# PSUM as one ring of eight places, and one drain for each pair of score tiles

## The chip, the cores and the metric

The kernel runs on one core of a Trainium2 chip. The metric is the time of one execution on the device, in microseconds; less is better. The kernel before takes 833.33 us, the median of 3 runs (831.85 to 833.4). Five engines work side by side and wait for one another through semaphores: TensorE (PE; its weight loads are listed as PEld), VectorE (DVE), ScalarE (ACT), GpSimd (POOL) and SyncE (SP), which issues most of the transfers. TensorE writes its products to PSUM, which has eight places (banks) of 512 fp32 numbers in each of 128 partitions; VectorE and ScalarE read them from there.

## The reference

All data are fp32; x is 4 batches of 512 tokens of 256 numbers, and the context has the same shape. Two layers follow each other:

```
x = x + tanh(g_xattn[0]) * attention0(layernorm(x), ctx)
x = x + tanh(g_ffn[0])   * ffn0(layernorm(x))        # weights rounded to -1, 0, 1
x = x + tanh(g_xattn[1]) * attention1(layernorm(x), ctx)
x = x + tanh(g_ffn[1])   * ffn1(layernorm(x))        # one of four experts a token
```

Each attention has 16 heads of 16 numbers: scores are q.k / 4, softmax over the 512 keys, then the weighted sum of the values. Layer 0 adds -0.1 |i - j| to the scores; in layer 1 queries, keys and values go through a relu. The part of interest here is the softmax: its maximum over the keys, and the exponentials.

## The kernel before

The attention of both layers is cut into 32 groups (layer, batch, half of the 256 columns, even or odd heads). A group holds four heads, each in a strip of 32 partitions: 16 for the head and some spare ones. A group has four units, so there are 128 units, and every unit does a quarter of two things:

- `maxima(v, pair)`: for one tile of 128 queries, the scores with queries on the partitions and the 512 keys along the row. Its two products, one for each head of the pair, go to two places of PSUM, and VectorE's `tensor_reduce` takes each one's maximum over the keys into a column of `m` (L517).
- `weights(u, pair)`: for one tile of 128 keys, the scores again with keys on the partitions and the 512 queries along the row. The queries carry their negative maximum in a spare row (`shifted` writes it there, from `m` turned by TensorE), so that the products are already shifted. ScalarE's `Exp` takes each of the two places to `p` (L532). In layer 0 GpSimd then multiplies one block by a decay (L535).

`scores(u, vs)` puts these together. A unit's four pairs form two quads: [maxima pair 0, weights pair 1], then [maxima pair 1, weights pair 0]. All four products of a quad are issued to TensorE, then its two drains to VectorE and ScalarE. The four use different strips of TensorE's rows, so they run side by side. The maxima run `LEAD` = 6 units ahead of the weights. A few quads hold two pairs of the same kind.

After each unit's scores `slot(u)` issues other work: every fourth unit `weighted` (the product of the exponentials with the values, L560) and `shifted`; between them jobs from `chains`, lists of steps with due times (projections, layer norms, the hidden layers of the first feed-forward, routing), up to a cost of `SLOT`. The order on TensorE, VectorE, ScalarE and GpSimd is the order in which the code issues the instructions. After the last unit comes the tail with the experts' tiles.

All products, of scores and of everything else, get their place of PSUM from `bank_psum` (L64). It takes a tile of one place from a pool with eight buffers, in turn. The framework that builds the program adds the waits: a product waits until the place's last readers are done, a reader waits for the place's writers, and two engines that read the same place are put in order.

Of the kernel before, what the change touches and what calls it, by code (L numbers as in the profile page):

```python
# [11 lines left out]
F32 = mybir.dt.float32  # L12
U32 = mybir.dt.uint32
AF = mybir.ActivationFunctionType
ALU = mybir.AluOpType
AX = mybir.AxisListType
PSUM = bass.MemoryType.PSUM
ET = mybir.EngineType

P = 128  # L20
# [9 lines left out]
SCALE = 1.0 / np.sqrt(DK)  # L30
# [21 lines left out]
def flamingo_kernel(ctx: ExitStack, tc: tile.TileContext, t: dict, out: bass.AP):  # L52
    nc = tc.nc
# [5 lines left out]
    wts = ctx.enter_context(tc.tile_pool(name="wts", bufs=2))  # L59
    dram = ctx.enter_context(tc.tile_pool(name="dram", bufs=1, space=bass.MemoryType.DRAM))  # L60
    sml = ctx.enter_context(tc.tile_pool(name="sml", bufs=4))
    ps = ctx.enter_context(tc.tile_pool(name="ps", bufs=8, space=PSUM))

    def bank_psum(name):  # L64
        return ps.tile([P, 512], F32, tag="bank", name=name)


    x = [const.tile([P, NT, D], F32, tag=f"x{b}", name=f"x{b}") for b in range(B)]
# [190 lines left out]
    def output_bias():  # L259


        bvm = made["bvm"]
        pb = bank_psum("pbv")[:, 0:D]
        for c in range(NC):
            nc.tensor.matmul(
                pb, lhsT=bvm[:, c, :], rhs=wo0[:, c, :], start=(c == 0), stop=(c == NC - 1)
            )
        nc.vector.tensor_tensor(bo0, bo0, pb, ALU.add)
        nc.gpsimd.tensor_scalar(bo0, bo0, gx0, None, ALU.mult)


    def quantize(flat, name, by_two):
# [12 lines left out]
        def limits():  # L285
            tot = bank_psum(f"qtot_{name}")
            nc.tensor.matmul(tot[:, 0:1], lhsT=ones, rhs=part[:, 0:1], start=True, stop=True)

            mean = sml.tile([P, 1], F32, tag="qmean", name=f"qmean_{name}")
            nc.vector.tensor_scalar(mean, tot[:, 0:1], 1.0 / (D * FF), 1e-5, ALU.mult, ALU.add)  # L290
            nc.vector.tensor_scalar(thr[:, 0:1], mean, 0.5, None, ALU.mult)
            nc.vector.tensor_scalar(thr[:, 1:2], mean, -0.5, None, ALU.mult)
# [82 lines left out]
    def transposed(src, dst, name, alone=False):  # L375

        for c in range(NC):
            pt = bank_psum(f"pt_{name}{c}")
            for n in range(NT):
                nc.tensor.transpose(pt[:, ts(n, P)], src[:, n, ts(c, P)], ident)  # L380
            (nc.scalar.copy if alone or c == 0 else nc.vector.tensor_copy)(dst[:, c, :], pt)
# [119 lines left out]
    def score(out_, lhs, rhs, i, n):  # L501
        r = slice(i * HP, (i + 1) * HP)
        nc.tensor.matmul(out_, lhsT=lhs[r, ts(n, P)], rhs=rhs[r, :], start=True, stop=True)  # L503

    def maxima(v, pair):

        g = groups[v // NT]
        n = v % NT
        pm = [bank_psum(f"pm{v}{pair}{i}") for i in range(2)]
        for i in range(2):  # L510
            score(pm[i], qs[g], ks[g], 2 * pair + i, n)
        m = m_sb[g[0]][g[3]]
        r = SPARE[g[3]]

        def drain():
            for i in range(2):
                nc.vector.tensor_reduce(m[:, n, 2 * pair + i, r : r + 1], pm[i], AX.X, ALU.max)  # L517

        return drain

    def weights(u, pair):

        g = groups[u // NT]
        kt = u % NT
        psc = [bank_psum(f"psc{u}{pair}{i}") for i in range(2)]
        for i in range(2):
            score(psc[i], ks[g], q2s[g], 2 * pair + i, kt)

        def drain():
            p = act.tile([P, 2, S], F32, tag="p", name=f"p{u}{pair}", bufs=10)  # L530
            for i in range(2):
                nc.scalar.activation(p[:, i, :], psc[i], AF.Exp, scale=SCALE)  # L532
            if g[0] == 0:
                d = p[:, :, ts(kt, P)]
                nc.gpsimd.tensor_tensor(d, d, dec.unsqueeze(1).to_broadcast([P, 2, P]), ALU.mult)  # L535
            ps_exp[u, pair] = p

        return drain

    def scores(u, vs):  # L540

        ms = [(maxima, v, pair) for v in vs for pair in range(2)]
        ws = [(weights, u, 1 - pair) for pair in range(2)] if 0 <= u < n_units else []
        while ms or ws:
            if ms and ws:
                quad = [ms.pop(0), ws.pop(0)]
            else:
                left = ms or ws
                quad = [left.pop(0), left.pop(0)]
            for drain in [f(w, pair) for f, w, pair in quad]:  # L550
                drain()
# [712 lines left out]
    for u in range(-NT, n_units):  # L1264
# [22 lines left out]
        if u in totals:  # L1287
            job, i = totals[u]
# [215 lines left out]
```

## Time and profile before

| | |
|---|---|
| median of the runs | 833.33 us |
| profiled execution | 831.85 us, of which the span from first to last instruction is 830.1 |
| mean granted TensorE clock | 0.994 |
| VectorE: maxima, L517 | 512 of 683 ns, 317.0 us |
| ScalarE: exponentials, L532 | 512 of 601 ns, 267.1 us |
| TensorE: score products, L503 | 2048 passes, 263.1 us (maxima) and 275.5 us (weights) |
| TensorE: exponentials with values, L560 | 1024 passes of 595 ns, 116.5 us |
| GpSimd: decay, L535 | 128 of 746 ns, 94.9 us |

The page lists for each group of instructions its line, engine, operation, what it writes and reads, how many there are, then its busy time and the mean time of one, and last the time for which the engine was idle just before, with what ended it. An fp32 product appears as two passes. TensorE's passes overlap, and their ends are modelled, so its busy time may hold short waits; the starts show them.

### The profile page before, as it was taken

The page shows a single profiled execution, that of the slowest core. Times are in us where ns is not written, and L with a number is a line of the kernel's source. Part 1 is how long each engine was busy: PE and PEld are TensorE (multiplying, and loading weights), DVE is VectorE, ACT ScalarE, POOL GpSimd, SP SyncE. Part 2 cuts the span into 40 slices and gives each one's busy share as a digit, 9 for nine tenths or more (in the row PEclk, how much of TensorE's full clock was granted, in tenths as well). Part 3 has the DMA queues.
Part 4 walks back from the last instruction along what each step waited for, and adds up shares of the span by engine and source line. Part 5 has one row for each costly group of instructions (what it writes and reads, how often), then busy time and mean ns, then how long its engine had stood idle before and what let it go on. Part 6 is the DMA issues. An engine that isn't in the chain of part 4 may idle for free. (4 is left out here: it accounts for less than half of the span.)

```text
span 830.1 us, 13595 instructions
## 1 busy us (share of the span) xinstructions
PE 805.9 (97%) x5220; PEld 450.6 (54%) x5220; DVE 565.7 (68%) x1258; ACT 430.2 (52%) x900; POOL 290.5 (35%) x453
## 2 busy tenths in 40 slices
PE   5999999999999999999999999999999999999995
PEld 3444444545454345644565444564444555899994
DVE  6768868765857686577854676557687764689443
ACT  2476655653546454455635566346756666533341
POOL 5548455624233253231011132002313431735722
PEclk9999999999999999999999999999999999999998
DMA  8200000000001000000000001000104222726820
GB/s 313 77 1 1 1 1 1 1 1 1 1 1 39 1 1 1 1 27 1 1 1 1 26 1 52 1 1 1 52 1 148 91 94 77 273 80 240 303 94 32
DMA packets 17712, 42.28 MB, mean 51 GB/s; under 512 B 2032, under 2 KB 12016, under 8 KB 15216
## 3 DMA queue, kind: packets, MB, share of 16 engines
q0 software_dynamic: 5104, 27.34, 9.4%
q1 hardware_dynamic: 12128, 13.54, 4.8%
q8 instruction: 41, 0.67, 0.3%
q10 hardware_dynamic: 416, 0.54, 0.2%
q14 instruction: 23, 0.19, 0.1%
HBM read 35.13 MB, written 6.29 MB: 50 GB/s over the span
## 5 line engine op out<-in xcount | busy, mean ns | idle before, releaser
L517 DVE TENSOR_REDUCE m<-pm 128x1 f32<-128x512 f32 x512 | 317.0, 683 | 109.1 <-PE psc L503 105.6
L532 ACT ACTIVATE p<-psc 128x512 f32<-128x512 f32 x512 | 267.1, 601 | 145.7 <-PE psc L503 143.5
L503 PE MATMUL psc<-q,k 32*128 32x512 f32 x1024 | 275.5, 624 | 0.0
L503 PE MATMUL pm<-k,q 32*128 32x512 f32 x1024 | 263.1, 617 | 1.5 <-ACT q L490 0.9
L535 POOL TENSOR_TENSOR p<-p,dec 128x256 f32<-128x256 f32 x128 | 94.9, 746 | 170.9 <-ACT p L532 170.9
L503 PEld LDWEIGHTS pm<-k,q 32*128 32x128 f32 x1024 | 92.8, 184 | 83.4 <-issue 48.1
L503 PEld LDWEIGHTS psc<-q,k 32*128 32x128 f32 x1024 | 105.7, 184 | 51.4 <-issue 27.7
L560 PE MATMUL po<-p,v 128*32 128x512 f32 x1024 | 116.5, 595 | 0.8 <-DVE m L517 0.8
L560 PEld LDWEIGHTS po<-p,v 128*32 128x32 f32 x1024 | 31.3, 109 | 80.9 <-issue 58.6
L1104 PE MATMUL pg<-xs,wg 128*128 128x128 f32 x608 | 71.6, 276 | 0.7 <-DVE m L517 0.7
L1104 PEld LDWEIGHTS pg<-xs,wg 128*128 128x128 f32 x608 | 69.8, 192 | 4.1 <-DVE m L517 1.7
L583 POOL TENSOR_TENSOR q<-q,mT 128x512 f32<-128x512 f32 x16 | 20.3, 1269 | 132.3 <-ACT mT L582 132.3
L1130 ACT ACTIVATE ha<-pg,wg 128x128 f32<-128x128 f32 x120 | 34.3, 368 | 52.5 <-PE pg L1104 52.5
L682 PE MATMUL ph<-xTf,w1q 128*128 128x512 f32 x128 | 60.0, 605 | 0.0
L566 ACT COPY oT<-po 128x512 f32<-128x512 f32 x32 | 18.7, 586 | 75.6 <-PE po L560 75.6
L1299 PE MATMUL pyf<-wo,ha 128*128 128x256 f32 x256 | 57.6, 379 | 0.0
L388 PE MATMUL py_f<-w2q,h 128*128 128x256 f32 x256 | 57.2, 381 | 0.0
L388 PEld LDWEIGHTS py_f<-w2q,h 128*128 128x128 f32 x256 | 48.0, 190 | 9.4 <-DVE m L517 3.0
L1299 PEld LDWEIGHTS pyf<-wo,ha 128*128 128x128 f32 x256 | 47.6, 190 | 5.9
L460 PE MATMUL pk<-cT,wk 128*128 128x512 f32 x68 | 35.3, 644 | 7.3 <-DMA cT<-in_ctxT_dram 7.3
L682 PEld LDWEIGHTS ph<-xTf,w1q 128*128 128x128 f32 x128 | 22.6, 189 | 30.3 <-issue 18.2
L393 DVE SCALAR_TENSOR_TENSOR x<-py_f,tg,x 128x512 f32<-128x512 f32 x8 | 6.0, 751 | 42.4 <-PE py_f L388 42.4
(259 smaller groups left out, 828.6 us busy)
## 6 DMA issues: line engine op xcount, KB each, us to landing
x<-in_x_dram SPq DMA_DIRECT2D x4, 512.0 KB, 8.5
rows_d<-xn_f SPq DMA_DIRECT2D x4, 512.0 KB, 3.0
rows_d<-x SPq DMA_DIRECT2D x4, 512.0 KB, 3.7
cT<-in_ctxT_dram SPq DMA_DIRECT2D x3, 512.0 KB, 9.6
w1q<-in_w_dram SPq DMA_DIRECT2D x1, 1024.0 KB, 8.8
w2q<-in_w_dram SPq DMA_DIRECT2D x1, 1024.0 KB, 11.2
wo<-in_wo_dram SPq DMA_DIRECT2D x2, 512.0 KB, 3.8
rows<-in_rows_dram SPq DMA_DIRECT2D x1, 640.0 KB, 9.2
```

Of the source, the lines that this page charges most:

```text
L388: nc.tensor.matmul(py[:, n, :], lhsT=operand(c, n0 + n), rhs=w[:, c, :], start=(c == 0), stop=(c == chunks - 1),)
L460: nc.tensor.matmul(pp, lhsT=attn_w[layer][w][:, c, ts(tt, P)], rhs=src[:, c, :], start=(c == 0), stop=(c == NC - 1),)
L503: nc.tensor.matmul(out_, lhsT=lhs[r, ts(n, P)], rhs=rhs[r, :], start=True, stop=True)
L517: nc.vector.tensor_reduce(m[:, n, 2 * pair + i, r : r + 1], pm[i], AX.X, ALU.max)
L532: nc.scalar.activation(p[:, i, :], psc[i], AF.Exp, scale=SCALE)
L535: nc.gpsimd.tensor_tensor(d, d, dec.unsqueeze(1).to_broadcast([P, 2, P]), ALU.mult)
L560: nc.tensor.matmul(po[i * HP : (i + 1) * HP, :], lhsT=v_sb[b % 2][0][:, kt, c0 : c0 + HP], rhs=ps_exp[NT * s + kt, i // 2][:, i % 2, :], s ...
L583: nc.gpsimd.tensor_tensor(q2s[g], qs[g], turned, ALU.subtract)
L682: nc.tensor.matmul(ph, lhsT=w1q[:, c, ts(f, P)], rhs=st["xT"][:, c, :], start=(c == 0), stop=(c == NC - 1),)
L1104: nc.tensor.matmul(ph[:, f, :], lhsT=w[:, c, ts(f2 * NF // 2 + f, P)], rhs=xs[j][:, c, :], start=(c == 0), stop=(c == NC - 1),)
L1130: nc.scalar.activation(ha[:, f, :], (ha if src is None else src)[:, f, :], AF.Gelu, bias=biases[j][:, fa : fa + 1],)
L1299: nc.tensor.matmul(py, lhsT=hs[j, f // 4][:, f % 4, :], rhs=wo1[f // 4][:, f % 4, :], start=(f == 0), stop=(f == NF - 1),)
```

## The change

PSUM becomes one tile, `ring`, of eight places. `bank_psum` hands out the places in turn, as before. `two_banks` takes two in turn and also returns one access pattern over both: two neighbours, or, where the first is place 7 and the second place 0, a pattern over place 0 and place 7 with a step of seven places (the pair is handed out in that order then, so that head and column still match). Each drain is one instruction over the two places: `tensor_reduce` writes two columns of `m`, and `Exp` writes all of `p`.

```diff
-    ps = ctx.enter_context(tc.tile_pool(name="ps", bufs=8, space=PSUM))
+    ps = ctx.enter_context(tc.tile_pool(name="ps", bufs=1, space=PSUM))
+
+    ring = ps.tile([P, 8, 512], F32, name="ring")
+    turn_of = [0]
 
     def bank_psum(name):
-        return ps.tile([P, 512], F32, tag="bank", name=name)
+        i = turn_of[0]
+        turn_of[0] = (i + 1) % 8
+        return ring[:, i, :]
+
+    def two_banks(name):
+
+        i = turn_of[0]
+        both = [bank_psum(name) for _ in range(2)]
+        if i == 7:
+            return both[::-1], ring[:, 0:8:7, :]
+        return both, ring[:, i : i + 2, :]
...
-        pm = [bank_psum(f"pm{v}{pair}{i}") for i in range(2)]
+        pm, both = two_banks(f"pm{v}{pair}")
         for i in range(2):
             score(pm[i], qs[g], ks[g], 2 * pair + i, n)
...
         def drain():
-            for i in range(2):
-                nc.vector.tensor_reduce(m[:, n, 2 * pair + i, r : r + 1], pm[i], AX.X, ALU.max)
+            nc.vector.tensor_reduce(m[:, n, 2 * pair : 2 * pair + 2, r], both, AX.X, ALU.max)
...
-        psc = [bank_psum(f"psc{u}{pair}{i}") for i in range(2)]
+        psc, both = two_banks(f"psc{u}{pair}")
         for i in range(2):
             score(psc[i], ks[g], q2s[g], 2 * pair + i, kt)
...
             p = act.tile([P, 2, S], F32, tag="p", name=f"p{u}{pair}", bufs=10)
-            for i in range(2):
-                nc.scalar.activation(p[:, i, :], psc[i], AF.Exp, scale=SCALE)
+            nc.scalar.activation(p, both, AF.Exp, scale=SCALE)
```

## The prediction

> **What bounds the kernel now.** I read the page's busy shares first, then its clock row and costliest groups.
>
> ```profile
> PE 805.9 (97%) x5220; PEld 450.6 (54%) x5220; DVE 565.7 (68%) x1258; ACT 430.2 (52%) x900; POOL 290.5 (35%) x453
> ...
> PEclk9999999999999999999999999999999999999998
> ...
> L517 DVE TENSOR_REDUCE m<-pm 128x1 f32<-128x512 f32 x512 | 317.0, 683 | 109.1 <-PE psc L503 105.6
> L532 ACT ACTIVATE p<-psc 128x512 f32<-128x512 f32 x512 | 267.1, 601 | 145.7 <-PE psc L503 143.5
> L503 PE MATMUL psc<-q,k 32*128 32x512 f32 x1024 | 275.5, 624 | 0.0
> L503 PE MATMUL pm<-k,q 32*128 32x512 f32 x1024 | 263.1, 617 | 1.5 <-ACT q L490 0.9
> ```
>
> TensorE is busy 97% of the span with almost no idle before its groups; VectorE and ScalarE idle, and what they idle for is the score products (105.6 and 143.5 us). So TensorE sets the time. Its busy time has modelled ends, though, and can hide short waits, so I turned to starts. The timeline of one unit, engine by engine (start, length, group):
>
> ```profile
> 404.26 0.70 PE L503 MATMUL pm<-k,q 32*128 32x512 f32 x2
> 404.28 0.70 PE L503 MATMUL psc<-q,k 32*128 32x512 f32 x2
> ...
> 405.24 0.59 PE L503 MATMUL pm<-k,q 32*128 32x512 f32 x2
> ...
> 406.35 0.70 PE L460 MATMUL pk<-cT,wk 128*128 128x512 f32 x1
> ...
> 405.42 2.48 DVE L517 TENSOR_REDUCE m<-pm 128x1 f32<-128x512 f32 x4 [0.18 <-PE psc L503]
> ...
> 405.56 2.07 ACT L532 ACTIVATE p<-psc 128x512 f32<-128x512 f32 x4 [2.75 <-PE psc L503]
> ```
>
> The first quad of four products starts at 404.26, the second 0.98 later at 405.24, without waiting for the drains of the first, which begin at 405.42 and 405.56 only. The job behind starts at 406.35, 1.11 after the second quad, while both drain engines are still at it. The eight places are what allows that: TensorE runs one unit ahead of its drains. Over all 256 quads the next work starts 0.97 after the quad's start at best; what lies above that sums to 39.5 us. That is all that better drains could give back.
>
> **Part 1: one instruction for two.** 256 reductions and 256 exponentials go (as built, 555 reductions become 299, 784 activations 528). In a row, reductions start every 0.598 us, so a pair took 0.598 + 0.683 = 1.28; the row of 128x512 against the 128x256 rows of VectorE (L1311 421 ns, L585 679 ns) gives about 1.04 ns an element, so one of 1024 elements takes 0.683 + 512 x 1.04 = 1.22. ScalarE: starts every 0.478, a pair 1.08; copies of 256 and 512 elements (389, 586 ns) and of 128 (281) give about 0.8 ns an element, so 0.601 + 0.41 = 1.01. Saved: some 0.06 a pair on each engine, 15 us of busy time each, on engines that are 68% and 52% busy: alone worth nothing on the path but a part of the 39.5 us. Against it the pair's first place comes free with its second, 0.55 later than now. The quad that reuses them mostly needs both; I cost this at nothing, between -10 and +10.
>
> **Part 2: the ring, where the pair is places 7 and 0.** Single places are still taken in turn, so a pair starts at any place. Where it starts at 7, the read is `ring[:, 0:8:7, :]`, whose first and last address enclose the whole ring. I looked up in the built program what each instruction waits for. A read of two neighbours waits for those two places' writers. A read of 7 and 0 is taken to touch all eight: it waits for the last read by the other drain engine, of whatever place, and for the quad's other products; the other drain engine's next read waits for it; and **the next TensorE instruction waits for it, whatever place that one writes**. I counted 65 such pairs, 36 reductions and 29 exponentials, spread over the attention (quads at 32 to 690 us of the span). At each, the unit's overlap above is gone, and TensorE stands until the drain is over. Behind the waiting product stands all of TensorE's queue, the bound of the kernel.
>
> A rule of the Trainium skill bears on this: "PSUM — Partial Sum Buffer", section "PSUM bank collisions raise a hardware error", asks that any two engines' accesses to one bank and quadrant be serialised, ScalarE's against VectorE's reads too. By that rule a wrapped pair would need to be ordered against places 7 and 0 alone, both old by then, and would cost nothing; the built program orders it against all eight. The row in before that shows an order of two readers of one place is `k` L474 waiting for `k` L472: 10.0 us in 8 times. The sum below goes by the program's waits; by the rule alone it would be 0.
>
> The price at the unit shown, with 0.05 us from a drain's end to what it releases (q of L496 ended at 411.71, the product that waited for its place started at 411.76):
> - Reduction of the first quad: 405.42 + 1.22 + 0.05 = 406.69 for the second quad, which started at 405.24: **1.45**.
> - Exponential of the first quad: it waits for that quad's reduction first: 406.69 + 1.01 + 0.05 = 407.75: **2.5**.
> - Reduction of the second quad: after the first (406.64) + 1.22 + 0.05 = 407.91 for the job, which started at 406.35: **1.55**.
> - Exponential of the second quad: 407.91 + 1.01 + 0.05 = 408.97: **2.6**.
>
> I made this sum at all 65 places, each with its own starts in the trace of before: 24 reductions ahead of a quad 36.6 us, 12 ahead of a job 18.4, 15 exponentials ahead of a quad 41.4 (one of 4.6 where VectorE is busy with the routing), 14 ahead of a job 36.3: **+133 us**. Of it comes back: after such a stand all places are free, so the small waits of the quads behind shrink; 29.3 of the 39.5 us lie at quads without a wrapped pair, and I take half, **-15** (between 0 and -29). If a drain of two took as long as two apart, 65 reductions (29 of them ahead of an exponential) and 29 exponentials cost 0.06 more each, +6.
>
> **Part 3: the clock.** Before never stands for long, except at the head, where the windows view shows (stretch, PE, PEld, DVE, ACT, POOL, then the granted clock):
>
> ```profile
> 21.86:25.28 3.42, 3.42 (x22) 1.58 (x15) 2.91 (x6) 2.16 (x5) 3.16 (x13) 1.00 0.99 333
> 25.28:28.69 3.41, 1.47 (x9) 1.16 (x8) 3.37 (x6) 0.00 (x0) 3.19 (x24) 1.00 0.03 6
> 28.69:32.10 3.41, 3.41 (x14) 1.59 (x15) 0.00 (x0) 0.59 (x1) 2.54 (x3) 0.50 0.03 7
> 32.10:35.51 3.41, 3.41 (x22) 1.29 (x15) 3.21 (x6) 3.12 (x8) 1.45 (x2) 1.00 0.00 0
> ```
>
> The reader is to see that TensorE stood 1.94 us of one stretch of 3.41 and ran the next one at half clock: about 1.7 us of work lost. The Trainium skill, "TensorE: Matmul & The Clock Gate", Part 1, lets the clock fall only after an idle window of some 3.4 us; by it no stand here (2.9 at most but for one) costs clock, and the change ends 28 us lower. By the row, a stand of about 2 us inside one stretch suffices. I take the row. A stand of 2.6 is cut by a stretch's boundary into two parts under 1.8 for 1.0 of 3.41 positions, so some 0.7 of them have 1.8 or more in one stretch; one of 1.5 never has. I take 0.65, and 1.5 us lost for each: 29 x 0.65 x 1.5 = **+28**. Ends: 0 by the rule; if stands of 1.5 trip it half the time too, 36 x 0.5 x 1.5 = 27 more.
>
> **What stays.** Order and amount of TensorE's work are the same; no DMA moves; the experts' tail after 690 us takes single places only and costs nothing more. GpSimd's decay (L535, 746 ns) starts after a pair as before.
>
> **Sum.** The profiled execution took 831.85 (span 830.1, so 1.75 around it), the fastest of the three, whose median is 833.33. 831.85 + 133 - 15 + 28 = 978; I say **977**.
>
> **Rivals.**
> - *Same waits, no clock loss.* For it: the skill's rule, and that score products and weight loads around a stand may count as activity. Against: the row above. 831.85 + 133 - 15 = 950.
> - *The stands are largely absorbed.* If most of the 65 waits are satisfied sooner, say because drains start with the quad's first product, half the sum: 831.85 + 66 - 15 = 883. For it: VectorE and ScalarE idle a third and a half. Against: those idle times are waits for the very products; nothing runs ahead of a TensorE that stands.
> - *Not slower.* The mechanism: the drains' saved 0.06 a pair and fewer instructions end the hidden waits at the places' release, 39.5 us at most: 831.85 - 39.5 = 792 if the wrapped reads cost nothing. It decides once a wrapped pair costs under 0.6 us (39.5 / 65). Against: one reduction alone is 1.22, and the instruction behind it on TensorE names it.
> - *The change doesn't do what it says*: the built program has 256 fewer instructions on each engine, so it does.
>
> **Numbers.** Stands with clock loss 0.62 (977, own range 960 to 1010), stands without 0.26 (950, from 935), absorbed 0.08 (883), not slower 0.04. The range 930 to 1020 takes in the first two: its low end is no clock loss with all 29 us back (831.85 + 133 - 29 = 936) and drains a little shorter, its high end nothing back and the clock lost at the short stands too (831.85 + 133 + 28 + 27 = 1020). What a measurement can tell from no change is about 0.2%, 1.7 us; slower than that 0.96, faster 0.03, within 0.01.
>
> **What would show it.** PE's share falls from 97% to some 85%, with idle before its groups, released by `m` and `p`, of 100 us and more; the group of reductions has 256 of about 1220 ns and that of exponentials 256 of about 1010; ScalarE gains a wait of `p` for `m` and VectorE one of `m` for `p`, which the waits view of before does not have; a stretch at half clock after many of ScalarE's wrapped pairs. I am wrong if TensorE's idle stays under 40 us, if the pairs' durations are far from these, or if the mean clock stays at 0.99 (then 950). A time under 834 would refute the stands.

## The result, and the profile after

The changed kernel takes 1022.61 us (median of 5 runs, 1020.23 to 1027.79), the kernel before 832.34 in the same five rounds: a ratio of 1.2289, with a 95% interval of 1.2269 to 1.2308. The forecast was 977 with a range of 930 to 1020: the sign and the place were right, but the time lies just above the range. The profiled execution was the slowest of the five, 1027.79 us with a span of 1026.1; the parts below are of that execution, against the 831.85 of before.

The page of the kernel after, busy shares, clock row (the granted clock in tenths, over 40 equal slices of the span) and the groups that answer to those shown of before:

```profile
PE 848.2 (83%) x5220; PEld 452.4 (44%) x5220; DVE 558.7 (54%) x1002; ACT 421.8 (41%) x644; POOL 289.3 (28%) x453
...
PEclk9999999989899899989999999999999899999998
...
L530 DVE TENSOR_REDUCE m<-ring 128x2 f32<-128x1024 f32 x256 | 305.6, 1222 | 248.6 <-PE ring L517 235.1
L544 ACT ACTIVATE p<-ring 128x1024 f32<-128x1024 f32 x256 | 256.5, 1022 | 272.5 <-PE ring L517 170.6
L517 PE MATMUL ring<-k,q 32*128 32x512 f32 x1024 | 270.5, 639 | 78.5 <-ACT p L544 40.3
L517 PE MATMUL ring<-q,k 32*128 32x512 f32 x1024 | 281.5, 649 | 0.3 <-DVE h L702 0.3
```

The drains of two have the durations of the sum (1222 ns for 1220, 1022 for 1010), and both drain engines are less busy than before. TensorE's busy share has fallen from 97% to 83%, and the products of the maxima now have 78.5 us of idle time in front of them where there were 1.5. The waits view names what ends it (engine and line, what it waited for, total, times, longest):

```profile
ACT p L544 <- DVE m L530: 97.8, 56, 4.2
...
PEld ring L517 <- ACT p L544: 54.1, 20, 5.3
PEld ring L517 <- DVE m L530: 53.8, 27, 2.9
...
PE ring L517 <- ACT p L544: 40.3, 15, 4.5
PE ring L517 <- DVE m L530: 37.3, 26, 2.0
```

The first row, exponentials that wait for maxima, did not exist before: two engines that read different heads' scores now take turns. The others are the score products and their weight loads, which wait for the drains' ends. The timeline of one unit shows the whole chain; its first quad's pair of exponentials lies in places 7 and 0. First the starts of its two quads in the kernel before:

```profile
144.94 0.70 PE L503 MATMUL pm<-k,q 32*128 32x512 f32 x2
...
145.92 0.59 PE L503 MATMUL pm<-k,q 32*128 32x512 f32 x2
```

Then the same unit in the changed kernel:

```profile
173.94 0.70 PE L517 MATMUL ring<-k,q 32*128 32x512 f32 x2
...
174.47 0.59 PE L517 MATMUL ring<-k,q 32*128 32x512 f32 x2
174.49 0.59 PE L517 MATMUL ring<-q,k 32*128 32x512 f32 x2
177.56 0.70 PE L517 MATMUL ring<-k,q 32*128 32x512 f32 x2 [2.48 <-ACT p L544]
...
175.14 1.23 DVE L530 TENSOR_REDUCE m<-ring 128x2 f32<-128x1024 f32 x1 [1.34 <-PE ring L517]
...
176.48 1.02 ACT L544 ACTIVATE p<-ring 128x1024 f32<-128x1024 f32 x1 [1.83 <-DVE m L530]
```

Before, the second quad starts 0.98 us behind the first. Now the first quad's last passes start at 174.47; the reduction runs to 176.37, only then the exponential starts, to 177.50, and the second quad, which writes neither of the two places, starts at 177.56, 3.62 behind the first. The wrapped exponential itself takes 1.02 us, like the others: what costs is the waiting, not the read.

**Where the 196 us went.** I compared, quad by quad, the time from a quad's first start to the start of TensorE's next work in both traces, then the time of the jobs between units. The clock loss is an estimate: time at half clock (a granted clock of 0.5, in stretches of 3.41 us) is priced at 0.42 us per us, which is what the jobs, the same work in both, give: they take 32.3 us more and have 77 us more of half clock in them.

| part | us more than before | of it clock |
|---|---|---|
| 65 quads with a wrapped pair | 137.8 | 2 |
| other second quads and the work behind them (97) | 26.3 | 5 |
| other first quads and the quad behind them (94) | -0.6 | 2 |
| jobs between the units | 32.3 | 32 |
| head and tail | 0.2 | 0 |

So some 136 us are stands (times in which TensorE waits), 19 a loss at quads without a wrapped pair, and 41 the clock.

### The profile page after: what moved, and what is told of

Read it like the earlier page. It is cut to its first block, busy times and chain, and to the rows that moved or that the text cites. A ratio compares the mean times of both kernels' runs of the same rounds, so it can differ in the third digit from the quotient of the medians.

```text
span 1026.1 us, 13209 instructions
## 1 busy us (share of the span) xinstructions
PE 848.2 (83%) x5220; PEld 452.4 (44%) x5220; DVE 558.7 (54%) x1002; ACT 421.8 (41%) x644; POOL 289.3 (28%) x453
## 5 line engine op out<-in xcount | busy, mean ns | idle before, releaser
L530 DVE TENSOR_REDUCE m<-ring 128x2 f32<-128x1024 f32 x256 | 305.6, 1222 | 248.6 <-PE ring L517 235.1
L544 ACT ACTIVATE p<-ring 128x1024 f32<-128x1024 f32 x256 | 256.5, 1022 | 272.5 <-PE ring L517 170.6
L517 PE MATMUL ring<-k,q 32*128 32x512 f32 x1024 | 270.5, 639 | 78.5 <-ACT p L544 40.3
L517 PE MATMUL ring<-q,k 32*128 32x512 f32 x1024 | 281.5, 649 | 0.3 <-DVE h L702 0.3
L517 PEld LDWEIGHTS ring<-k,q 32*128 32x128 f32 x1024 | 86.3, 189 | 189.3 <-issue 76.4
L572 PE MATMUL ring<-p,v 128*32 128x512 f32 x1024 | 127.7, 643 | 30.0 <-ACT p L544 15.5
L517 PEld LDWEIGHTS ring<-q,k 32*128 32x128 f32 x1024 | 94.6, 189 | 36.5 <-issue 19.0
L694 PE MATMUL ring<-xTf,w1q 128*128 128x512 f32 x128 | 70.4, 694 | 10.7 <-ACT p L544 8.5
L1116 PE MATMUL ring<-xs,wg 128*128 128x128 f32 x608 | 73.1, 279 | 0.5 <-DVE m L530 0.5
L1116 PEld LDWEIGHTS ring<-xs,wg 128*128 128x128 f32 x608 | 71.5, 196 | 3.7 <-issue 1.9
L694 PEld LDWEIGHTS ring<-xTf,w1q 128*128 128x128 f32 x128 | 26.3, 219 | 48.3 <-issue 30.0
```

The lines of the kernel that those rows point to most:

```text
L530: nc.vector.tensor_reduce(m[:, n, 2 * pair : 2 * pair + 2, r], both, AX.X, ALU.max)
L544: nc.scalar.activation(p, both, AF.Exp, scale=SCALE)
L572: nc.tensor.matmul(po[i * HP : (i + 1) * HP, :], lhsT=v_sb[b % 2][0][:, kt, c0 : c0 + HP], rhs=ps_exp[NT * s + kt, i // 2][:, i % 2, :], s ...
L694: nc.tensor.matmul(ph, lhsT=w1q[:, c, ts(f, P)], rhs=st["xT"][:, c, :], start=(c == 0), stop=(c == NC - 1),)
L1116: nc.tensor.matmul(ph[:, f, :], lhsT=w[:, c, ts(f2 * NF // 2 + f, P)], rhs=xs[j][:, c, :], start=(c == 0), stop=(c == NC - 1),)
```

## The experiments

My theory after the result: false waits of the 65 wrapped pairs (waits on places that the instruction does not touch), their clock loss, and the later release of a pair's first place. Rivals: drains of two are dear wherever they are (A); the ring itself, as one tile, costs waits (B); the rest of the loss lies in later drains and added waits on all engines (C); any stand costs clock alike (D). There are 512 pairs, 256 on each drain engine, of which 65 are wrapped; the expectations of the first, fourth and last kernel speak of 256 in all. So rival A's number there is too high for the fourth (832 + 190 x 65/512 = 856) and too low for the first and last; no conclusion turns on it. Every kernel ran beside the kernel before on the same chip; the median of the kernel before was 832.20 us for the first four and 830.32 for the last four.

**Two instructions at wrapped pairs only.**

```diff
+        around = turn_of[0] == 7
         pm, both = two_banks(f"pm{v}{pair}")
...
-            nc.vector.tensor_reduce(m[:, n, 2 * pair : 2 * pair + 2, r], both, AX.X, ALU.max)
+            if not around:
+                nc.vector.tensor_reduce(m[:, n, 2 * pair : 2 * pair + 2, r], both, AX.X, ALU.max)
+            else:
+                for i in range(2):
+                    nc.vector.tensor_reduce(m[:, n, 2 * pair + i, r : r + 1], pm[i], AX.X, ALU.max)
```

(and the same for the exponentials)

> The ring and the drains of two stay; only the 65 pairs on places 7 and 0 are drained by two instructions, each of one place. Theory (false waits of the wrapped pairs, plus their clock loss, plus the later release of a pair's first place): stands of 138 us and the clock loss go, the late release of some 20 us stays: 850 to 860 us, clock back at 0.99, no stretches at half clock between 40 and 800 us. Rival A (drains of two are dear wherever they are): 191 of the 256 stay, so at least 950 us. Rival B (the ring itself, not the pairs): still about 1020.

Measured: 875.93 us, ratio 1.0524 (1.0507 to 1.0542), clock 0.995. One stretch at half clock is left, at 668 us, where I had expected none. Removing the 65 wrapped reads takes 147 us away, and 447 of 512 drains of two remain, so rival A is out, and B could explain 44 us at most. But 44 us are left, twice what I expected. They lie behind second quads: 49.0 us more than before at the 123 of them. In the kernel after, this loss shows only at second quads that start at an even place; the units of the others have a stand, behind which every place is free, and so the stands had hidden it. So 147 us went, and not the 177 of stands and clock.

**The ring alone**, all drains of one place (condition `if False` in both drains).

> The ring in place of the pool, all drains of one place as before. Theory: nothing but the tracking of places differs, so the time of before, 830 to 835 us. Rival B (waits that come from one tile of eight places): well over 850 us.

Measured: 841.70, ratio 1.0116 (1.0099 to 1.0133). That is above my range and 9.5 us above the kernel before, so the ring does cost something, but far less than the "well over 850" of rival B. The comparison quad by quad gives the cause: 12 jobs start about 0.57 us later, each behind a first quad whose maxima lie in places 7 and 0. `two_banks` hands these out as 0, 7, so the loop drains place 0 first and 7 second, while the job behind the unit takes 7, the older one. It is the late release again, made by an order; the kernel with place 7 first, below, tests this. (Two jobs near the routing, later by 1.9 and 1.3 us, are most of the rest; I did not look for their cause.)

**First maxima apart.** As the first experiment, with one place per instruction also for the maxima of pair 0, which stand first in a usual unit (`if not around and pair == 1`).

> As the kernel with two instructions at wrapped pairs, and also the maxima of pair 0, which stand first in a unit's first quad, by two instructions. The place of the first of them is the one that the first job behind the unit takes. Theory: the late release goes, so 828 to 838 us, and the job behind a unit's second quad starts about 1.0 to 1.1 us after it again. Rival C (the rest of the loss is the drains' later starts, or more waits on all engines): stays at 850 or more.

Measured: 845.20, ratio 1.0158 (1.0141 to 1.0175), 31 us below the first experiment and 7 above the expected range (the profiled execution, which has no stretch at half clock before the tail, took 841.89). The same unit in both, behind its second quad; first with the pair in one reduction (the first experiment), then with two:

```profile
165.03 0.59 PE L517 MATMUL ring<-k,q 32*128 32x512 f32 x2
...
166.67 1.92 PE L582 MATMUL ring<-p,v 128*32 128x512 f32 x15 [0.58 <-DVE m L532]
...
165.30 2.36 DVE L532 TENSOR_REDUCE m<-ring 128x2 f32<-128x1024 f32 x2 [0.38 <-PE ring L517]
```

```profile
159.94 0.59 PE L517 MATMUL ring<-k,q 32*128 32x512 f32 x2
...
160.96 0.64 PE L582 MATMUL ring<-p,v 128*32 128x512 f32 x4
...
160.12 1.29 DVE L535 TENSOR_REDUCE m<-ring 128x1 f32<-128x512 f32 x2 [0.30 <-PE ring L517]
```

The second quad starts at 165.03 and at 159.94, the job behind it 1.64 and 1.02 later. The job needs one place, the first of the unit, and waits for it alone; two reductions free it at about half time. Rival C is out: 344 drains of two are still there, and the work behind the 123 second quads, which starts 49.0 us later in all than before in the first experiment, starts 10.4 us later here. Of these 10.4, 6.7 lie at the 21 second quads at place 3, where the order of places 7 and 0 is left as it was.

**Wrapped pairs alone.** The converse of the first (`if around`): 65 drains of two, all others of one.

> The converse: only the 65 wrapped pairs are drained by one instruction, all others by two. Theory: 138 us of stands and about 40 us of clock loss stay, the late release goes: 995 to 1012 us, clock about 0.95. Rival A (drains of two are dear wherever they are): 65 of 256 are left, so 832 + 190 x 65/256 = 880 us.

Measured: 1008.65, ratio 1.2109 (1.2070 to 1.2149), in the range, with 32 stretches at half clock in the profile. An eighth of the pairs carries nearly all of the loss; rival A is out by 150 us.

**Only the 36 wrapped maxima, and only the 29 wrapped exponentials** (`if around` in one of the two drains, `if False` in the other).

> The ring; only the 36 wrapped pairs of maxima are drained by one instruction, all else by two. Theory (a stretch of 3.41 us loses half its clock behind a stretch in which TensorE stood for about half, 1.4 to 2.0 us): stands of 36 x 1.6 = 58 us, too short to trip the clock often, at most 10 stretches at half clock: 892 to 910 us. Rival D (any stand costs clock alike): 30 x 36/65 = 17 stretches, 915 us or more.

> The converse: only the 29 wrapped pairs of exponentials are drained by one instruction. Theory: from the 842 us of the ring alone, 29 stands of 2.85 us (the reduction before it is two of one place here) make 82 us, and most of them trip the clock: 18 to 26 stretches at half clock, 1.5 us each: 945 to 965 us. Rival D: 13 stretches, 940 us or less.

Measured: 896.77, ratio 1.0791 (1.0757 to 1.0826), with 7 stretches at half clock in the profiled execution; and 945.91, ratio 1.1407 (1.1365 to 1.1449), with 20. Of the 7, two have no wrapped pair ahead of them; of the 20, one is the stretch at the head that the kernel before has too. So 36 stands of some 1.6 us gave 5, and 29 of some 2.8 gave 19: the clock goes more by how long TensorE stands than by how often. The counts are of one execution each and vary (over four executions the granted clock was 0.978 to 0.989 in the first kernel, 0.949 to 0.961 in the second), but these ranges do not meet. Rival D, which asked for 17 and 13, is out.

**Place 7 first.** The third experiment, and a wrapped pair is handed out and drained as 7, then 0.

```diff
         if i == 7:
-            return both[::-1], ring[:, 0:8:7, :]
+            return both, None
```

> As the kernel with the first maxima apart, and at a wrapped pair place 7 is written and drained first, place 0 second. Theory (the job behind a unit takes the oldest place, 7, which the order 0, 7 frees last: 12 jobs of 0.57 us in the ring alone): 830 to 838 us, level with the kernel before or up to 4 us above it. Rival (the remaining 9 to 13 us come from the ring's tracking): 841 or more.

Measured: 837.03, ratio 1.0069 (1.0056 to 1.0083), in the range, though 6.7 us above the kernel before where I had allowed 4. Against the kernel before in the same rounds, the third experiment had 13.0 us, so the order was worth some 6, about the 12 x 0.57 of the ring alone. Most of what is left in its trace is the two jobs near the routing (1.9 and 1.3 us) and one more stretch at half clock. It is the best version with drains of two that I ran, and it does not beat the kernel before.

**All pairs in one instruction, none wrapped.** A pair that would start at 7 starts at 0; place 7 is left out that time.

```diff
     def two_banks(name):
 
+        if turn_of[0] == 7:
+            turn_of[0] = 0
         i = turn_of[0]
         both = [bank_psum(name) for _ in range(2)]
-        if i == 7:
-            return both[::-1], ring[:, 0:8:7, :]
```

> All 256 pairs are drained by one instruction; a pair that would start at place 7 starts at 0, and 7 is left out that time. Theory: no stands and no clock loss, the late release stays, at more units than with two instructions at wrapped pairs, since the skip makes the next pairs start at even places: 875 to 895 us, mean clock above 0.99. Rival A (drains of two are dear wherever they are): about 1000 us.

Measured: 927.82, ratio 1.1170 (1.1153 to 1.1187), clock 0.988. Rival A is out again, but the time is 33 us above my range, and the clock below the 0.99 that I expected. The loss lies behind the 123 second quads, 97.4 us in all. With one place left out, a unit has seven for its eight score tiles, so a product inside the unit waits for a drain of the same unit. The waits view of this kernel:

```profile
PE ring L517 <- DVE m L530: 22.7, 47, 1.1
PE ring L572 <- DVE m L530: 8.9, 17, 1.0
```

The 16 second quads at places 5, 6, 0, 1, which follow a quad at 1 to 4 and so take place 1 again, hand over to the job 1.57 us later each, 25 us in all. The rest of the excess I did not take apart.

## Why the prediction was wrong

The sum was +133 for the stands, -15 for waits that shrink behind them, 0 for the later release and +28 for the clock: 145.5 and so 977. The profiled execution has 196.

- **TensorE sets the time, and the wrapped pairs stop it: right.** The experiments that remove them or leave them alone show it. The other reading that the prediction weighed, waits for places 7 and 0 alone, would have made it 0. The size was right too: 133 against some 136 measured. By case: ahead of a quad 1.53 forecast and 1.62 measured for a reduction, 2.76 and 2.81 for an exponential; ahead of a job 1.53 and 1.65, 2.59 and 2.63.
- **The later release of a pair's first place: the step that failed.** The prediction said "The quad that reuses them mostly needs both; I cost this at nothing". The work behind a unit's second quad is most often not a quad but a job, which needs a single place, and that is the first place of the first pair. At the 62 second quads that start at even places it cost 24.4 us, 0.4 each; where no stand hides it, in the first experiment, it is 49.0 at all 123. Both are above the bound of 10 that the prediction gave it. The third experiment, which gives that one place back early, takes 31 us from the first. For quads behind quads the prediction was right: -0.6 us at 94 of them.
- **What comes back behind a stand: also off.** I took half of 29.3 us of hidden waits. In the 39 quads that follow a stand in their own unit the gain is 0.3 us, or some 5 without the half clock in them. Together these two terms stand at +19 where the sum had -15: 34 of the 50 us.
- **The clock: mechanism right, size off.** To take the row of the trace, and not the rule of the Trainium skill ("TensorE: Matmul & The Clock Gate", Part 1: an idle window of some 3.4 us), was right: 30 stretches at half clock instead of one, and only one of them behind a stretch in which TensorE was idle throughout. Mis-sized was the share of stands that lose clock: 25 of the 29 long stands have a stretch at half clock behind them, three of these two in a row, so 28 where the sum had 19; and of the short ones, of which "one of 1.5 never has", two do (where they are alone, they gave five stretches). With the long stands alone the profiled execution had 19, the number put, so the share is not the same in every run; why it is higher with both is open. 29 more stretches at some 1.4 us each make 41 us where the sum had 28.
- **The range** ended at 1020 because it let the clock go wrong, but not the release: its own bound of 10 us was left out of the high end, which would have been 1030 with it.
- **The rivals.** "Same waits, no clock loss" (950) fails by the clock row. "Absorbed" (883) and "not slower" (a wrapped pair under 0.6 us) fail alike: 137.8 us over 65 wrapped pairs are 2.1 each, slightly more than summed.
- **The signs**: TensorE's share was to fall to some 85% (83), idle time by `m` and `p` over 100 us (it is), drains of 1220 and 1010 ns (1222, 1022), and a wait of `p` for `m` (97.8 us). The wait of `m` for `p` that it also named is hardly there: 1.1 us in 3 times.

## What to carry to other kernels

A buffer that is handed out in turn can, as here, be dear to read in pairs when a read's pattern encloses places that it doesn't touch: look at what the instruction after such a read waits for, in the built program, before any duration. Merging two drains saves little (0.06 us of 1.28 here) and delays the release of the first place by about half of the merged drain (0.55 us of 1.22); ask who takes that place next, since a consumer of one place pays where a consumer of both doesn't. Where TensorE sets the time and has stands of two or three microseconds, as here, price the clock that it loses behind them too, and put every cost that was set to nothing into the range.

## What the runs showed of the hardware

The clock fell behind stretches in which TensorE stood for only a part. The windows view of the kernel after, cut at the boundaries of its clock stretches (columns as before; the first number behind the length is TensorE's busy time, the third from the end the granted clock):

```profile
93.65:97.06 3.41, 1.05 (x10) 0.19 (x2) 2.39 (x2) 1.95 (x2) 1.62 (x2) 1.00 0.00 0
97.06:100.47 3.41, 3.26 (x16) 1.22 (x16) 1.07 (x1) 1.11 (x2) 0.73 (x1) 0.50 0.00 0
...
288.20:291.62 3.42, 1.62 (x8) 0.30 (x4) 3.38 (x5) 1.64 (x2) 0.72 (x1) 1.00 0.00 0
291.62:295.03 3.41, 2.86 (x16) 0.92 (x20) 1.63 (x6) 0.41 (x1) 2.19 (x4) 0.50 0.00 0
...
329.16:332.57 3.41, 1.45 (x4) 0.73 (x5) 0.79 (x1) 1.02 (x1) 1.07 (x2) 1.00 0.00 0
332.57:335.99 3.42, 3.42 (x17) 1.43 (x18) 1.73 (x3) 0.78 (x1) 0.00 (x0) 1.00 0.23 79
335.99:339.40 3.41, 2.02 (x11) 0.65 (x6) 2.85 (x3) 1.40 (x2) 0.72 (x1) 1.00 0.23 74
339.40:342.82 3.42, 3.42 (x7) 1.28 (x5) 0.69 (x1) 0.65 (x1) 0.73 (x1) 0.50 0.00 0
```

Idle for 2.36 and 1.80 of 3.41 us, TensorE gets half the clock in the next stretch. Over the whole trace, 27 stretches at full clock were followed by one at half; their idle time was 1.39 us or more, in 25 of them 1.74 or more. The last four rows show that the boundary isn't sharp in these numbers: 1.96 idle cost nothing, 1.39 did, and 20 stretches with 1.39 or more kept the clock behind them. Idle time is not the whole of it either. The kernel without wrapped pairs has four stretches at half clock, one alone and three in a row, and next to no idle time ahead of either group; the first:

```profile
562.63:566.05 3.42, 3.41 (x13) 0.98 (x8) 3.07 (x3) 3.10 (x7) 1.72 (x2) 1.00 0.10 37
566.05:569.46 3.41, 3.41 (x5) 1.24 (x5) 0.00 (x0) 0.93 (x1) 1.11 (x1) 0.50 0.75 255
```

TensorE's ends are modelled, so its true idle time may differ; what the hardware counts as activity is left open.
